# A four-layer graph network on one core: attention weights of layers 1 and 2 as the larger of a row factor and a node factor

## The chip, the cores and the metric

The kernel runs on one core of a Trainium2 chip. The metric is the device time of one execution in microseconds (us); a verdict compares medians of several executions of the kernel before and the kernel after on the same chip. The core has the engines PE (TensorE matmul, with PEld for its weight loads), DVE (VectorE), ACT (ScalarE) and POOL (GpSimd), and SP, which here only issues DMA transfers. Each engine works through its own queue in order. SBUF is the on-chip memory, PSUM the accumulators that PE writes.

## What is computed

128 graphs of 128 nodes with 128 features pass through four residual layers, each of which begins with a layer norm and a relu. `adj` holds 0 or 1, is symmetric and has a full diagonal. The change touches layers 1 and 2 alone:

```python
# layer 1, for each graph and each of 8 heads of 32 values
e   = leaky_relu(f1[:, None] + f2[None, :], 0.2)
att = softmax(where(adj > 0, e, -9e15), axis=-1)
hp  = elu(att @ h)                  # all heads side by side: xc, 256 values
h2  = xc @ W2
e2  = leaky_relu(g1[:, None] + g2[None, :], 0.2)
out = elu(softmax(where(adj > 0, e2, -9e15)) @ h2) + h_in
# layer 2
e   = leaky_relu((h @ a1) + (h @ a2).T, 0.2)
out = elu(softmax(where(adj > 0, e, -9e15)) @ h)
```

Layer 0 scores every pair of nodes, layer 3 is an attention with a bilinear score for each of 8 edge types, of which only 0 and 1 occur.

## The kernel before

The program has three stages. Stage A (profile time 0 to about 1230 us) makes layer 0's pair features. Stage B (to about 2045 us) reads them back, makes layer 0's scores and its attention, and stores `y`. Stage C, the function `layers`, finishes layer 0 and does layers 1, 2 and 3; it is the part that is changed. It exists twice, as the two arms of a run-time branch (lines 1358 to 1361): `layers(True)` where every adjacency entry is 0 or 1, `layers(False)` otherwise. The word that decides it, `types`, is made by `edge_types` in stage B from `squares`.

Stage C takes 4 graphs at a time (a group, `GC = 4`), so 32 groups, and a tile of one group has 128 partitions (nodes) by 4 x 128 values. `group(g)` is a generator that yields, step by step, the engine, an assumed cost in us, and the buffers taken and freed. `in_order` (line 54) plays all groups against these costs, with up to `UNDER_WAY = 6` of them open, and thereby fixes the order of the instructions of PE, ACT, DVE and POOL (`ORDERED`). The order is written out once; at run time each queue follows it and waits by semaphores. SP's order is not fixed by hand.

For one group before the change:

- `edges` turns the adjacency into a bf16 mask of 0 and -1 (POOL cast L1046, PE transpose L1050, DVE L1058). `with_bias` and `with_bias3` are additions on POOL (L1063, L1067). `normal_relu` is the layer norm: DVE statistics, a power on POOL (L948), DVE L951, ACT L955.
- Layer 1's heads, for each of the 4 graphs (`head_attention`): PE adds row and node terms in PSUM as an outer product of bf16 triples (L1081) and a mask term of 2^53 (L971); ACT takes the exponential twice, of the sum (L1090) and of 0.2 times it (L1091); DVE takes the larger of the two (L975 in `bounded`); PE multiplies the weights of each head with that head's values and a column of ones (L1104); DVE divides by the sum that the ones give (L1110, L1111). The bf16 triples come from DVE (L1196 to L1199, L1207).
- Layer 1's second attention and layer 2's (`single_head`) do the same with one head over the whole group: a score in PSUM (L1255, or L1281 and L1283, and L971), two exponentials (L986 or L983), the larger (L975), PE (L1019), DVE (L1026, L1028), and the elu (`positive` L1009, L998, L1002).
- The sum of the normed and the raw layer input, `x1h`, is a DVE addition (L1213).
- Layer 3 picks the score by edge type with `copy_predicated` (L1330), then two exponentials, DVE (L1336), PE (L1019), DVE (L1348), and SP stores the result (L1349). SP also loads four inputs for every group (L1039).

The tiles of the attention weights are `w` (128 x 1024, 11 buffers) for the heads and `t` (128 x 512, 28 buffers) for nearly everything else.

Of the kernel before, what the change touches and what calls it, by code (L numbers as in the profile page):

```python
# [9 lines left out]
F32 = mybir.dt.float32  # L10
# [8 lines left out]
P = 128  # L19
# [12 lines left out]
UNDER_WAY = 6  # L32
C_T, C_W, C_V, C_O, C_M = 28, 11, 3, 6, 7
C_KEPT = {"ps": 1, "t": 6, "w": 3, "v": 1}
# [6 lines left out]
SLOPE = 0.2  # L41
FAR = 2.0**53
# [120 lines left out]
def kernel(ctx: ExitStack, tc: tile.TileContext, x, adj, w, out):  # L163
# [57 lines left out]
    w2g = cst("w2g", [P, 2, P + 2])  # L221
# [18 lines left out]
    with tc.tile_pool(name="wload", bufs=2) as wl, tc.tile_pool(  # L240
# [21 lines left out]
        nc.vector.memset(fw, 0.0)  # L262
        nc.scalar.dma_start(w1c, w["L1_gnn_W1"].rearrange("h f d -> f h d"))
        a1b = wl.tile([P, NH, 2 * DH], F32, tag="a1b", name="a1b")
        nc.scalar.dma_start(a1b, bcast(w["L1_gnn_a1"], 0, P))
        for m in range(2):
# [7 lines left out]
            )  # L274

# [24 lines left out]
        for s in range(2):  # L300
# [4 lines left out]
            nc.vector.tensor_copy(w2g[:, :, P + s], gw)  # L305
# [4 lines left out]
        nc.gpsimd.dma_start(a2c, w["L2_gnn_a2"])  # L310

# [56 lines left out]
    h_d = [dram.tile([P, GB, P], F32, tag=f"h{g}", name=f"h{g}") for g in range(NB // GB)]  # L368

# [63 lines left out]
    with tc.tile_pool(name="h_pool", bufs=1) as h_pool, tc.tile_pool(name="pairs", bufs=B_V) as b_v:  # L433
# [198 lines left out]
        with tc.tile_pool(name="b2", bufs=2) as b2p, tc.tile_pool(name="b_s", bufs=2, space=PSUM) as b_s, tc.tile_pool(  # L632
# [6 lines left out]
            squares = b2p.tile([P, n_parts], F32, tag="squares", name="squares", bufs=1)  # L639

# [145 lines left out]
            def attention(k, g, u):  # L786
# [19 lines left out]
                mx = b2p.tile([P, GB], F32, tag="mx", name="mx")  # L806
                nc.vector.tensor_reduce(mx, pl, AX.X, ALU.max)
                e = b2p.tile([P, GB, P], F32, tag="e", name="e")
                nc.vector.tensor_tensor(e, pl, bcast(mx, 2, P), ALU.subtract)
                yield ACT, 0.65, "", ""  # L810
# [41 lines left out]
            def edge_types():  # L852
# [5 lines left out]
                nc.vector.tensor_scalar(odd_p, odd_p, GB * P / 4.0, None, ALU.is_gt)  # L858
                yield PE, 0.3, "pb", ""
# [16 lines left out]
            to_see, to_norm = set(range(n_parts)), set(range(n_parts))  # L876
# [25 lines left out]
    def layers(simple):  # L902

        with tc.tile_pool(name="c_in", bufs=3) as c_in, tc.tile_pool(
            name="c_t", bufs=C_T
        ) as c_t, tc.tile_pool(name="c_w", bufs=C_W) as c_w, tc.tile_pool(name="c_v", bufs=C_V) as c_v, tc.tile_pool(
            name="c_s", bufs=6
        ) as c_s, tc.tile_pool(name="c_ps", bufs=4, space=PSUM) as c_ps, tc.tile_pool(
            name="c_pz", bufs=2, space=PSUM
# [19 lines left out]
            def tile_v(name):  # L929
                return c_v.tile([P, GC, P + 3], F32, tag="v", name=name, bufs=C_O)  # L930
# [46 lines left out]
            def single_head(z, own, bias, values, ones_at, after, out):  # L977
# [13 lines left out]
                yield PE, 0.9, "pz", "t v"  # L991
                po = weighted(p, values, ones_at + 1)
                yield DVE, 0.8, "t", "pz"
# [10 lines left out]
                )  # L1004

# [25 lines left out]
            loaded = {0: early}  # L1031
# [10 lines left out]
            def edges(ad, res):  # L1042
# [8 lines left out]
                if not simple:  # L1051
# [84 lines left out]
            def group(g):  # L1136
# [80 lines left out]
                for i in range(GC):  # L1217
                    yield "fork", head_attention(i, f1d, fl, mask, vals, xh)
# [182 lines left out]
```

The softmax here doesn't subtract the row's maximum and nothing guards it: scores larger than these inputs give would overflow.

## Time and profile before

| What | Value |
|---|---|
| Runs of the kernel before | 3104.69, 3115.43, 3116.11 us; median 3115.43 |
| Span of the profiled execution | 3120.3 us |
| Mean granted TensorE clock | 0.969 |
| Stage C, first yl (L1148) to the end | 2044.5 to 3120.3 us |
| DMA in stage C, 2100 to 2900 us | 13% of the engines' time, 39 GB/s |
| DMA in stage B, slices 17 to 25 of 40 | 382 to 406 GB/s |
| SP's issues in stage C | 0.32 to 0.46 us each in the steady part |
| A 256 KB load or store in stage C, issue to landing | 2.4 to 3.1 us (medians by tensor) |

How to read it: the busy time of an engine counts the time in which at least one of its instructions is under way. A group of instructions is named by its line, engine, operation and tiles, "x" is how many there are, and a shape such as 128x512 is partitions by elements. A line that is a helper's (L948, L955, L971, L975, L1019, L1028) stands for several places in the program. An engine's instructions overlap a little, so the length of a run of equal instructions is read from the time line and not from the mean times the count.

### The profile page before, as it was taken

Reading aid. Unit: us, or ns where it says so; the run is one execution under the profiler, and the core shown is the slowest. Engines: PE = TensorE matmul, PEld = TensorE weight load, DVE = VectorE, ACT = ScalarE, POOL = GpSimd, SP = SyncE. Lnnn points to the kernel's source line nnn. Section 1 sums busy time; section 2 is a strip of 40 time slices with the busy share of each in tenths; the row PEclk is TensorE's granted clock in tenths of the full one; section 3 lists DMA queues with packets and bytes.
Section 4 is the critical chain, followed back from the end, with each engine's and each line's share of the span. In section 5 each row is a group of like instructions: output and inputs, shape, how many; then the busy total and the mean of one; then the engine's idle time right before and its main releaser. Section 6 shows DMA issues by size and latency. Waiting matters only on the chain.

```text
span 3120.3 us, 47393 instructions
## 1 busy us (share of the span) xinstructions
PE 2854.7 (91%) x17526; PEld 1595.5 (51%) x17577; DVE 2655.0 (85%) x4722; ACT 2624.7 (84%) x3050; POOL 1504.5 (48%) x972
## 2 busy tenths in 40 slices
PE   7999999999999998888888878879999999999997
PEld 3344433444334343233333333367777777787786
DVE  7999999999999998777776868768787787887886
ACT  5999999999999998887877878657877777887786
POOL 7999999999999996011111111221222222222202
PEclk9999999999999999999998989989999999999999
DMA  3655556655555550999999999630111111111000
GB/s 127 254 232 244 238 228 251 248 231 228 244 241 228 234 241 18 385 381 395 383 406 400 384 382 393 248 97 11 45 48 35 48 38 45 42 42 38 18 1 22
DMA packets 149247, 606.52 MB, mean 194 GB/s; under 512 B 14272, under 2 KB 97536, under 8 KB 118288
## 3 DMA queue, kind: packets, MB, share of 16 engines
q1 hardware_dynamic: 136128, 568.48, 46.1%
q0 software_dynamic: 10848, 33.60, 3.0%
q8 instruction: 143, 2.34, 0.3%
q10 hardware_dynamic: 2032, 1.31, 0.2%
q14 instruction: 96, 0.79, 0.1%
HBM read 322.74 MB, written 280.61 MB: 193 GB/s over the span
## 4 chain that ended last, share of the span: by engine, by line
PE 40%; DVE 32%; issue 10%; ACT 8%; POOL 6%; DMA 2%; POOLq 0%; SPq 0%; DVEq 0%; another core or an unknown queue 0%; ACTq 0%
PE ph L573 10%; DVE six L588 9%; DVE d L553 8%; PE pa L1104 6%; PE sc L707 5%; POOL d L556 4%; PE po L1019 2%; DVE p L975 2%; DMA s<-us 2%; PE ps L1123 1%; PE pl L799 1%; PE pp L1116 1%; PE pl L801 1%; PE z L971 1%; DVE v L428 1%
## 5 line engine op out<-in xcount | busy, mean ns | idle before, releaser
L556 POOL TENSOR_TENSOR d<-he 128x2016 f32<-128x2016 f32 (+1 forms) x288 | 1021.4, 3571 | 67.2 <-PE ph L573 60.2
L573 PE MATMUL ph<-d,w1T 128*64 128x512 f32 (+1 forms) x4096 | 929.0, 595 | 36.3 <-DVE us L515 13.8
L559 ACT ACTIVATE d<-d 128x2016 f32<-128x2016 f32 (+1 forms) x352 | 675.6, 1923 | 16.8 <-POOL d L556 16.7
L588 DVE BATCH_NORM_STATS2 six<-v 128x6 f32<-128x512 f32 (+1 forms) x1024 | 624.4, 669 | 6.5 <-ACT v L583 6.2
L573 PEld LDWEIGHTS ph<-d,w1T 128*64 128x64 f32 x4096 | 312.1, 136 | 539.7 <-issue 393.4
L583 ACT COPY v<-ph 128x1024 f32<-128x1024 f32 (+1 forms) x512 | 509.7, 1029 | 28.2 <-PE ph L573 26.9
L553 DVE TENSOR_TENSOR d<-he,pt 128x2048 f32<-128x2048 f32 (+1 forms) x224 | 505.4, 2257 | 2.4 <-PE ph L573 2.4
L948 POOL TENSOR_TENSOR rs<-ve,nhalf 128x4 f32<-128x4 f32 x96 | 119.2, 1241 | 737.8 <-DVE ve L945 479.5
L428 DVE SCALAR_TENSOR_TENSOR v<-v 128x1528 f32<-128x1528 f32 x256 | 433.9, 1741 | 34.2 <-ACT v L662 33.6
L662 ACT ACTIVATE v<-v,h_bi,h_sc 128x1528 f32<-128x1528 f32 x256 | 413.3, 1664 | 6.9 <-DVE h_bi L420 6.9
L707 PE MATMUL sc<-v,w_slide 128*32 128x512 f32 (+1 forms) x1536 | 324.9, 600 | 19.1 <-DVE v L428 18.7
L1104 PE MATMUL pa<-vals,p 128*128 128x99 f32 (+2 forms) x2048 | 251.7, 278 | 11.4 <-DVE p L975 7.8
L1104 PEld LDWEIGHTS pa<-vals,p 128*128 128x128 f32 x2048 | 246.9, 196 | 29.1 <-DVE p L975 11.7
L707 PE MATMUL sc<-v,w_line 128*32 128x504 f32 x512 | 260.7, 591 | 0.0
L707 PE MATMUL sc<-r,w_relu 128*32 128x504 f32 x512 | 258.2, 586 | 0.0
L975 DVE SCALAR_TENSOR_TENSOR p<-p,q 128x1024 f32<-128x1024 f32 (+1 forms) x192 | 206.9, 1084 | 50.1 <-ACT q L1091 24.4
L573 PE MATMUL ph<-both,us 128*64 128x512 bf16 x1920 | 237.7, 380 | 0.0
L573 PEld LDWEIGHTS <-us 128*64 128x64 bf16 x1920 | 125.9, 110 | 146.9 <-issue 92.2
L1090 ACT ACTIVATE p<-z 128x1024 f32<-128x1024 f32 x128 | 133.1, 1040 | 34.4 <-PE z L971 34.0
L669 ACT ACTIVATE r<-v,h_bi,h_sc 128x1008 f32<-128x1008 f32 x128 | 157.6, 1231 | 0.0
L707 PEld LDWEIGHTS sc<-v,w_slide 128*32 128x32 f32 x1536 | 65.6, 109 | 162.7 <-DVE v L428 87.0
L799 PE MATMUL pl<-u,ident 128*128 128x512 f32 x64 | 49.2, 860 | 96.6 <-POOL u L792 96.6
(275 smaller groups left out, 4490.4 us busy)
## 6 DMA issues: line engine op xcount, KB each, us to landing
v<-v SPq DMA_DIRECT2D x240, 2032.0 KB, 8.6
xg<-in_x SPq DMA_DIRECT2D x64, 256.0 KB, 3.1
ht<-h SPq DMA_DIRECT2D x64, 256.0 KB, 5.7
u<-s POOLq DMA_DIRECT2D x16, 768.0 KB, 11.8
h<-he SPq DMA_DIRECT2D x32, 256.0 KB, 2.7
adj<-in_adj SPq DMA_DIRECT2D x32, 256.0 KB, 2.9
adj<-in_adj POOLq DMA_DIRECT2D x32, 256.0 KB, 8.2
y<-yt POOLq DMA_DIRECT2D x32, 256.0 KB, 6.2
```

What stands on the lines that cost most here:

```text
L428: engine.scalar_tensor_tensor(out, v, slope, v, ALU.mult, ALU.max)
L553: nc.vector.tensor_tensor(dv, later, own, ALU.max if larger else ALU.subtract)
L556: nc.gpsimd.tensor_tensor(dv, later, own, ALU.subtract)
L559: nc.scalar.activation(d[:, 0 : 4 * n], d[:, 0 : 4 * n], AF.Abs)
L573: nc.tensor.matmul(ph[64 * a : 64 * a + 64, t, 0:n], wt, x_, start=part == 0, stop=not larger or part == 3,)
L583: nc.scalar.copy(v.rearrange("p (t e) -> p t e", t=2), ph[:, :, 0:n])
L588: nc.vector.bn_stats(made["six"][:, 2 * q + t, :], v[:, t * n : t * n + n])
L662: nc.scalar.activation(part, part, AF.Identity, bias=h_bi, scale=h_sc)
L669: nc.scalar.activation(made["r"][:, 0:n], part, AF.Relu, bias=h_bi, scale=h_sc)
L707: nc.tensor.matmul(sc[rows, 0:n], wz[:, 31 - k : 63 - k], z, start=begins and q < NQ, stop=ends and q != NQ - 1, tile_position=(0, rows.st ...
L975: nc.vector.scalar_tensor_tensor(p, p, FLOOR, q, ALU.max, ALU.max)
L1104: nc.tensor.matmul(pa_all[:, h * (DH + 1) : h * (DH + 1) + n], p[:, h, :], vals_all[:, e : e + n], start=True, stop=True,)
```

## The change

In the general arm nothing of substance changes. In the arm for adjacencies of 0 and 1:

The weight exp(leaky_relu(f1 + f2)) is the larger of exp(f1) exp(f2) and exp(0.2 f1) exp(0.2 f2). Divided by what depends on the row alone, exp(0.2 f1), and by exp(f2), which is instead multiplied into the values, it is max(exp(0.8 f1), exp(-0.8 f2)): the larger of a factor of the row and a factor of the node. The row sum divides by the same thing, so the softmax is unchanged. The kernel after computes it so:

- `exp_rows`: one small product gives the row terms and the node terms of a group (PE), ACT takes one exponential of it, SP stores the 128 x 128 result `x` to DRAM (`rows_d`), and `exp_cols` transposes it (PE) and copies the node factors out (ACT).
- The row factors are needed along the free axis on all partitions. SP reads them back from DRAM with a partition step of 0: for the heads a 128 x 1024 tile for each graph (`one_graph`, tag `R`, 9 buffers), for the other two attentions a 128 x 512 tile for each group (`one_head`).
- DVE takes the larger of that tile and the node factors, broadcast along the row. POOL multiplies by the mask, now 0 and 1 in f32. PE multiplies with the values, which POOL (`scaled_values`, `scaled_nodes`) or ACT (`second`) has multiplied by exp(f2).
- For layer 1's second attention ACT takes the exponential of 3 columns, and SP stores the row factor from SBUF as single elements into `rows_d[1]`, in place of `exp_rows`.
- `x1h` is added on POOL (`added`). `copy_predicated` uses the f32 mask.
- An empty row would now have a sum of 0. Stage B therefore keeps every row's largest score (`tops`), and `edge_types` sends the program into the general arm where one of them is below NEG/2; `types` is thus made after the last of these maxima.
- `UNDER_WAY` is 7, and the simple arm has its own numbers of buffers and its own assumed costs.

```diff
-UNDER_WAY = 6
-C_T, C_W, C_V, C_O, C_M = 28, 11, 3, 6, 7
-C_KEPT = {"ps": 1, "t": 6, "w": 3, "v": 1}
+UNDER_WAY = 7
+GENERAL_ROOM = {
+    "ps": 4, "pz": 2, "t": 28, "w": 11, "vals": 3, "f": 3, "v": 6, "mask": 7,
+}
+GENERAL_KEPT = {"ps": 1, "t": 6, "w": 3, "v": 1}
+SIMPLE_ROOM = {
+    "ps": 4, "pz": 2, "t": 26, "w": 6, "vals": 3, "v": 6, "mask": 7, "R": 9, "x": 4,
+}
+SIMPLE_KEPT = {"ps": 1, "t": 6, "w": 2, "v": 1}
...
+                mx = tops[:, g * GB : g * GB + GB]
...
+                to_top.remove(g)
+                if not to_top:
+                    yield "done", "tops"
...
+                yield "after", "tops"
+                yield DVE, 0.5, "", ""
+                low = b2p.tile([P, 1], F32, tag="low", name="low", bufs=1)
+                nc.vector.tensor_reduce(low, tops, AX.X, ALU.min)
+                nc.vector.scalar_tensor_tensor(odd_p, low, NEG / 2.0, odd_p, ALU.is_lt, ALU.max)
...
+            def attended(p, values, ones_at, after, out):
+                yield PE, 0.95, "pz", "t v"
                 po = weighted(p, values, ones_at + 1)
-                yield DVE, 0.8, "t", "pz"
+                yield DVE, 0.9, "t", "pz"
...
+            def one_head(g, k, rows, values, after, out):
+                yield DMA, 0.7, "t", ""
+                p = tile_t("p")
+                nc.sync.dma_start(p, rows)
+                yield "after", ("cols", g, k)
+                yield DVE, 0.7, "", ""
+                nc.vector.tensor_tensor(p, p, bcast(values[:, :, P + 1], 2, P), ALU.max)
+                yield "after", ("mask", g)
+                yield POOL, 0.95, "", ""
+                nc.gpsimd.tensor_tensor(p, p, masks[g], ALU.mult)
+                yield "after", ("values", g, k)
+                yield from attended(p, values, P, after, out)
+            def exp_rows(g, k, hT, weights, cols_of, scale, frees):
+                yield PE, 0.45, "ps", frees
+                pf = c_ps.tile([P, P], F32, tag="ps", name="pf")
+                for i in range(GC):
+                    nc.tensor.matmul(
+                        pf[32 * i : 32 * i + 32, :], weights, hT[:, i, :],
+                        start=True, stop=True, tile_position=(0, 32 * i),
+                    )
+                yield ACT, 0.35, "x", "ps"
+                x = c_v.tile([P, P], F32, tag="x", name="x", bufs=room["x"])
+                nc.scalar.activation(x, pf, AF.Exp)
+                yield DMA, 0.1, "", ""
+                nc.sync.dma_start(rows_d[k][g], x)
+                yield "fork", exp_cols(g, k, x, cols_of, scale)
+            def exp_cols(g, k, x, cols_of, scale):
+                yield PE, 0.2, "ps", "x"
+                px = c_ps.tile([P, P], F32, tag="ps", name="px")
+                nc.tensor.transpose(px, x, ident)
+                yield ACT, 0.3, "", "ps"
+                dst, src = cols_of(px.rearrange("p (g r) -> p g r", g=GC))
+                nc.scalar.copy(dst, src)
+                yield "done", ("cols", g, k)
+                yield from scale(g)
+            def rows_of(g, k):
+                rd = rows_d[k][g]
+                return bass.AP(tensor=rd.tensor, offset=rd.offset, ap=[[0, P], [32 * P, GC], [1, P]])
...
+                if simple:
+                    yield ACT, 0.6, "mask", "ps"
+                    mask = c_in.tile([P, GC, P], F32, tag="mask", name="mask", bufs=room["mask"])
+                    nc.scalar.copy(mask, pad)
+                    masks[g] = mask
+                    yield "done", ("mask", g)
...
+            def one_graph(i, g, cols, vals, xh):
+                yield DMA, 1.3, "R", ""
+                p = c_r.tile([P, NH, P], F32, tag="R", name="R")
+                rd = rows_d[0][g]
+                nc.sync.dma_start(
+                    p, bass.AP(tensor=rd.tensor, offset=rd.offset + 32 * P * i, ap=[[0, P], [1, NH * P]])
+                )
+                yield "after", ("cols", g, 0)
+                yield DVE, 1.25, "", ""
+                nc.vector.tensor_tensor(p, p, bcast(cols[:, 0, i, :], 2, P), ALU.max)
+                yield "after", ("mask", g)
+                yield POOL, 1.95, "", ""
+                nc.gpsimd.tensor_tensor(p, p, bcast(masks[g][:, i, :], 1, NH), ALU.mult)
+                yield "after", ("values", g, 0)
+                yield PE, 1.9, "ps", "R"
+                yield from normal_heads(i, p, vals, xh)
+            def scaled_values(g, cols, vals):
+                yield "after", ("vals", g)
+                yield POOL, 1.95, "", ""
+                by_head = vals.rearrange("p g h d -> p (g h) d")
+                nc.gpsimd.tensor_tensor(
+                    by_head, by_head,
+                    bcast(cols[:, 1].rearrange("p g h -> p (g h)"), 2, DH + 1), ALU.mult,
+                )
+                yield "done", ("values", g, 0)
+            def added(got, h1, x1):
+                yield POOL, 0.95, "t", "t t"
+                got["x1h"] = tile_t("x1h")
+                nc.gpsimd.tensor_tensor(got["x1h"], h1, x1, ALU.add)
+            def scaled_nodes(g, hv):
+                yield POOL, 0.95, "", ""
+                nc.gpsimd.tensor_tensor(
+                    hv[:, :, 0:P], hv[:, :, 0:P], bcast(hv[:, :, P], 2, P), ALU.mult
+                )
+                yield "done", ("values", g, 2)
...
+            def many_heads(g, h1, x1, h1T, vals):
+                got = {}
+                yield "fork", added(got, h1, x1)
+                cols = c_v.tile([P, 2, GC, NH], F32, tag="cols", name="cols")
+                yield from exp_rows(
+                    g, 0, h1T, fe, lambda px: (
+                        cols,
+                        px[:, :, NH : 3 * NH].rearrange("p g (k h) -> p k g h", h=NH),
+                    ), lambda _: scaled_values(g, cols, vals), "t",
+                )
+                xh = tile_w("xh").rearrange("p (g a) (b d) -> p g (a b) d", g=GC, d=DH)
+                for i in range(GC):
+                    yield "fork", one_graph(i, g, cols, vals, xh)
+                yield "join",
+                return got["x1h"], xh
...
+            def second(g, xcT, x1h, x2):
+                yield PE, 1.9, "pz v", "w"
+                h2 = tile_v("h2")
+                ph2 = by_graph(psum2("ph2"))
+                for i in range(GC):
+                    for s in range(2):
+                        nc.tensor.matmul(
+                            ph2[:, i, 0 : P + 3], xcT[:, GC * s + i, :], w2g[:, s, 0 : P + 3],
+                            start=s == 0, stop=s == 1,
+                        )
+                yield ACT, 0.3, "", ""
+                nc.scalar.activation(h2[:, :, P : P + 3], ph2[:, :, P : P + 3], AF.Exp)
+                yield "fork", one_head_rows(g, h2, x1h, x2)
+                yield ACT, 1.5, "", "pz"
+                for i in range(GC):
+                    nc.scalar.activation(
+                        h2[:, i, 0:P], ph2[:, i, 0:P], AF.Identity, scale=h2[:, i, P : P + 1]
+                    )
+                yield "done", ("values", g, 1)
+                yield "join",
+            def one_head_rows(g, h2, x1h, x2):
+                yield DMA, 0.3, "", ""
+                rd = rows_d[1][g]
+                nc.sync.dma_start(
+                    bass.AP(tensor=rd.tensor, offset=rd.offset, ap=[[1, P], [32 * P, GC]]),
+                    h2[:, :, P + 2],
+                )
+                yield "done", ("cols", g, 1)
+                yield from one_head(g, 1, rows_of(g, 1), h2, x1h, x2)
...
+                if simple:
+                    yield from exp_rows(
+                        g, 2, h2T, ae, lambda px: (hv[:, :, P : P + 2], px[:, :, 1:3]),
+                        lambda _: scaled_nodes(g, hv), "t",
                     )
-                masked(z, lambda: mask)
-                x3 = []
-                yield from single_head(z, None, shift2, hv, P, x2, x3)
+                    yield from one_head(g, 2, rows_of(g, 2), hv, x2, x3)
+                    yield "join",
...
-                    sel = by_type.pop(1)
-                    nc.vector.copy_predicated(sel, mask.bitcast(I16), by_type.pop(0))
+                    sel = by_type.pop(0)
+                    nc.vector.copy_predicated(sel, masks.pop(g).bitcast(I32), by_type.pop(1))
```

`normal_heads` is the part of `head_attention` from the product with the values on, unchanged, and `attended` that of `single_head`. The weights `fe`, `ae` and `w2g`, prepared at the start of the program, get the factors 0.8 (`RISE`) and -0.8, with some ten small DVE instructions more.

## The prediction

> **What bounds the kernel now.** I read the busy times of the stretch 2100 to 2900 us first, where stage C runs evenly, then the groups of instructions there by form, then the waits, then the time line around single POOL instructions. The stretch (us, busy time and count of PE, PEld, DVE, ACT, POOL, then granted clock, DMA share, GB/s):
>
> ```profile
> 2100.00:2900.00 800.00, 754.26 (x5646) 620.69 (x5686) 642.40 (x1735) 627.14 (x1117) 177.07 (x239) 0.98 0.13 39
> ```
>
> PE is busy for 94% of it, DVE 80%, ACT 78%, POOL 22%. The groups give the pace:
>
> ```profile
> L1104 PEld LDWEIGHTS pa<-vals,p 128*128 128x128 f32 x1568 | 190.6, 197 | 23.2 <-DVE p L975 9.9 <-issue 4.1 <-ACT val L1325 2.2
> L975 DVE SCALAR_TENSOR_TENSOR p<-p,q 128x1024 f32<-128x1024 f32 x97 | 123.1, 1272 | 19.7 <-ACT q L1091 19.1
> L1090 ACT ACTIVATE p<-z 128x1024 f32<-128x1024 f32 x98 | 101.8, 1039 | 28.1 <-PE z L971 27.7
> ```
>
> L1090 runs 4 times for a group, so 98 of them are 24.5 groups, and one takes 800 / 24.5 = 32.65 us; 32 take 1045 of stage C's 1076 us. For a group PE is busy 30.8, DVE 26.2, ACT 25.6, POOL 7.2 us. PE sets the pace. POOL has room, which its longest waits show too:
>
> ```profile
> POOL rs L948 <- DVE ve L945: 396.4, 48, 20.1
> DVE ri L1110 <- PE pa L1104: 37.2, 32, 4.1
> ```
>
> But POOL's room isn't free. Two stretches of the time line (start, length, engine):
>
> ```profile
> 2585.14 1.27 POOL L1063 TENSOR_TENSOR xg<-xg,bt_bc 128x512 f32<-128x512 f32 x1
> 2585.14 2.35 DVE L975 SCALAR_TENSOR_TENSOR p<-p,q 128x1024 f32<-128x1024 f32 x1 [2.65 <-ACT q L1091]
> ...
> 2416.90 1.21 DVE L975 SCALAR_TENSOR_TENSOR p<-p,q 128x1024 f32<-128x1024 f32 x1
> 2416.93 2.31 POOL L1063 TENSOR_TENSOR xg<-xg,bt_bc 128x512 f32<-128x512 f32 x1
> 2418.24 0.69 DVE L1028 TENSOR_TENSOR xh<-po,ri 128x512 f32<-128x512 f32 x1
> ```
>
> Where both start together, DVE's 1.22 us instruction takes 2.35: it ends 1.08 after POOL's. Where DVE is 0.03 us ahead, POOL's 1.27 takes 2.31 and ends 1.13 after DVE's. So a POOL tensor operation and a DVE operation with two SBUF inputs exclude each other, each for its length less some 0.14 us. L1028, with one input in PSUM, runs its usual 0.69 beside POOL. POOL's power L948 hardly holds anything: an L975 that began 0.41 us into one, at 2168.90, took 1.22.
>
> **The change, engine by engine, for one group.**
>
> *PE* loses L1081 and L971 (4 graphs x 4 x 0.215, the spacing in the time line, = 3.4), the score of the second attention (8 x 0.111 + 0.2 = 1.1), that of layer 2 (2 x 0.43 + 8 x 0.111 + 0.2 = 2.0) and the old row terms (0.6); it gains two row products and two transposes (2 x 0.55 = 1.1). 30.8 - 6.0 = 24.8.
>
> *ACT* loses eight exponentials of 1.04 (8.3), eight of 0.385 (3.1), two of 0.70 (1.4) and a copy (0.6); it gains the mask copy (0.6), three small exponentials and two column copies (some 0.3 each: 1.4) and four scalings of 0.39 (1.6). 25.6 - 13.4 + 3.6 = 15.8.
>
> *DVE* loses L975 (4 x 1.22 + 2 x 0.68 = 6.2), the chain L1196 to L1207 (3.1), L1213 (0.7), L1058 and L1262 (0.6); it gains the larger-of, 4 x 1.21 + 2 x 0.69 = 6.2, the same size as L975. 26.2 - 10.6 + 6.2 = 21.8.
>
> *POOL* has no row of 128x1024, nor one that multiplies two full tiles. Its rows:
>
> ```profile
> L1063 POOL TENSOR_TENSOR xg<-xg,bt_bc x32: 1262/1274/2317, 2045.2 to 2940.3; 128x512 f32<-128x512 f32 x32
> L792 POOL TENSOR_TENSOR u<-u x32: 715/717/2237, 1311.3 to 2022.8; 128x256 f32<-128x256 f32 x32
> L488 POOL TENSOR_TENSOR ln_xn<-ln_xn,ln_rs x32: 1038/1040/1042, 22.7 to 1159.9; 128x512 f32<-128x512 f32 x32
> L556 POOL TENSOR_TENSOR d<-he x288: 3547/3557/3616, 29.3 to 1225.3; 128x2016 f32<-128x2016 f32 x95, 128x2048 f32<-128x2048 f32 x49
> ```
>
> (Shortest, median, longest in ns.) L1063 and L792, both operands read in full, give (1262 - 715) / 256 = 2.13 ns an element and 0.17 us beside. L488 and L556, one operand repeated along the row, give (3557 - 1040) / 1504 = 1.67 ns and 0.18. The mask product reads both in full: 1024 x 2.13 ns + 0.17 = 2.35 us, between 1.90 (the repeated operand's rate) and 2.52 (twice L1063). So 4 x 2.35 + 2 x 1.27 (`one_head`) + 1.27 (`added`) + 1.95 (`scaled_values`, 1056 elements, repeated) + 1.04 (`scaled_nodes`) = 16.2, less two memsets of 0.1; POOL has 23.2 us in place of 7.2. The change assumes 1.95 and 0.95 for these products in its order of work.
>
> [...]
>
> *What excludes what.* DVE holds for five of 128x1024 (four larger-of, L1228) x 1.08, nine of 128x512 (two larger-of, L428, L1009 and L1002 twice, L1336, L1348) x 0.55, three small L951: 10.5 us, 17 instructions. POOL holds for 4 x 2.21 + 2 x 1.13 + 1.81 + 1.13 + 0.90, L1063 and L1067 2 x 1.13, L1046 0.47, powers 0.3: 18.0. Together 28.5 us, more than PE's 24.8. This is the new bound. At the 94% that PE reaches today it is 28.5 / 0.943 = 30.2 us. From DVE's side: an instruction finds POOL holding with a chance of 18.0 / 30.4 = 0.6 and then waits 0.84 us (half of the sum of POOL's squared holds, 30.5, over 18.0); 17 x 0.6 x 0.84 = 8.6, and 21.8 + 8.6 = 30.4. I take 30.5.
>
> *SP.* Its issues go from 5 to 14 for a group, 14 x 0.4 = 5.6 us, in one queue: behind a row load that waits for the landing of its store stand the inputs, the other groups' rows and the output. Landing: a 256 KB store 2.4 us; single elements 4.2 (256 of them, from `own_row`), so 4.2 to 8.4 for the 512 here; a row load of 512 KB between 4.6 (`a1b`, 256 KB, one source to all partitions) and 8.6 (`v`, 2032 KB). The bytes, 3.9 MB a group, are 127 GB/s against 390 in stage B. I cost all this at nothing within the stage, because 9 tiles of `R` hold two groups and 7 groups are open; without that cover it is the second rival. At the end of the program nothing covers it: the last group passes two row trips one after the other, (4.2 + 3.1 + 0.7 + 1.3) against 4.4 for L1255 to L975, and (0.8 + 2.4 + 3.1 + 0.7 + 1.3) against 4.1: 9 us.
>
> *Before the stage.* `types` is written at 2019.15 now and SP's first load follows 1.1 later. The last L807 starts at 2031.83, so `types` moves to about 2034.6 and SP to 2035.7; its 12 loads end some 8.6 later, when ACT, at 2044.5, begins the first L1148. Hidden by the norm of `y` up to there; 0 to 6 us, I take 2. The weights' ten small DVE instructions at 0.15 to 0.2: 1 us.
>
> *Sum.* 32 x (30.5 - 32.65) = -69, +9, +2, +1: 3120.3 - 57 = 3063 on the profiled execution's scale. Its span is 5 us above the runs' median, so 3058; I say **3060**. Ends: with 1.90 for the mask product the holds are 26.7, 28.3 us a group, 2988; on the other side the next paragraph.
>
> **The rivals.**
>
> *DVE and POOL in each other's way, slower.* The order fixed by hand knows nothing of the exclusion and has POOL's products too short, so POOL runs late, DVE's queue stands at a larger-of or an elu while what follows could run, and POOL in turn finds no input. DVE has 11.3 us of work that needs no exclusion. My 30.5 means that 82% of it falls in POOL's holds. With half, a group takes 21.8 + 18.0 - 5.6 = 34.2 us: 3115 + 12 + 50 = 3177. It decides against the change from 32.3 us on (32 x 0.37 = the 12 us of the other terms), that is, below 67%. For it: L951 is drawn out to 0.55 to 1.22 us already. Against: only SBUF-to-SBUF work is hit.
>
> *Row trips bind.* Six open groups at 32.65 us are 196 us for one group now. Three trips of at least 2.4 + 4.6 add 21, the longer POOL steps some 8: 225 / 7 open groups = 32.1 us, 3110, no change. Against it: much of the 196 is queueing, which shrinks.
>
> *Exclusion matters little, PE stays the bound.* 24.8 / 0.943 = 26.3 us: 3115 + 12 - 203 = 2924. It needs POOL's product at 1.4 us or below, under every row.
>
> That the program takes the general arm is excluded by the full diagonal: no row is empty, and `types` stays 0.
>
> **How the numbers follow.** Exclusion at 29 to 31.9 us a group (3010 to 3103): 0.52, time 3060. The slower rival 0.30, the trips 0.10, PE 0.08. The range leaves out PE's 0.08 and the upper third of the slower rival: 2975 to 3185; the likeliest case's own is 3010 to 3103. Half a per cent, 15 us, is about what can be told from no change: faster needs 31.8 us or less, most of the first case and PE's; slower 32.8, most of the second. That is 0.53 faster, 0.12 same, 0.35 slower.
>
> **What would show it.** POOL's 128x1024 products near 2.35 us alone and longer beside DVE; the larger-of at 1.21 alone and up to 3.4 behind one; DVE and POOL each over 90% busy in the stretch, PE near 80%. Wrong: PE still above 93%, POOL's busy time below 65%, or SP's queue behind the longest waits of DVE.

## The result, and the profile after

| | Median, us | Runs |
|---|---|---|
| before | 3112.05 | 3104.69 to 3116.11 |
| after | 3839.47 | 3822.14 to 3854.19 |

The ratio is 1.2335, 95% interval 1.2286 to 1.2384: the change makes the kernel 727 us slower. The profiled execution of after has a span of 3852.4 us. Stage C begins about where it did (first yl at 2046.15 us, before at 2044.5), so the loss lies inside it: (3852.4 - 2046) / 32 = 56.4 us a group, where the same sum gives (3120.3 - 2044.5) / 32 = 33.6 before.

The stretch of after that was shown of before, with the same columns:

```profile
2100.00:2900.00 800.00, 451.37 (x2881) 386.26 (x2880) 447.32 (x845) 243.00 (x522) 391.76 (x242) 0.75 0.31 70
```

PE falls from 94% to 56%, and no other engine takes its place: DVE 56%, ACT 30%, POOL 49%, the DMA engines 31%. Nothing is full, so something makes everything wait. The granted clock is lower too, 0.75 in place of 0.98. The page's chain of waits says who (shares of the whole span, stages A and B included):

```profile
DMA 29%; DVE 27%; PE 22%; issue 9%; POOL 7%; ACT 5%; SPq 1%; POOLq 0%; DVEq 0%; ACTq 0%
DMA e<-h 15%; DMA p<-e 9%; PE ph L600 8%; DVE six L615 7%; DVE d L580 6%; PE sc L735 4%; POOL d L583 4%; DVE R L1231 3%; DMA e<-x 2%; DMA s<-us 1%; PE pa L1208 1%; PE pl L827 1%; PE po L1113 1%; PE pl L829 1%; DVE nb L992 1%
```

`e<-h` is the store of layer 1's second attention: 512 row factors, as single elements of 4 bytes, from the column of `h2` into `rows_d[1]` (L1399). `p<-e` is the load (L1059) that reads them, or those of layer 2, back to all partitions. Together they set 24% of the whole program (some 920 us), about half of stage C. The time line of after around one such trip, all engines:

```profile
2628.53 0.36 SPq L1399 DMA_DIRECT2D e<-h  x1
...
2636.54 0.69 ACT L1523 ACTIVATE dstT<-pd,kb 128x512 f32<-128x512 f32 x1 [0.41 <-PE pt L1004]
2637.13 0.58 ACT L1007 COPY hTc<-pt 128x512 f32<-128x512 f32 x1
2649.81 0.36 SPq L1059 DMA_DIRECT2D p<-e  x1
...
2658.91 0.69 DVE L1062 TENSOR_TENSOR p<-p,h 128x512 f32<-128x512 f32 x1 [26.29 <-DMA p<-e]
2659.52 0.15 DVE L992 SCALAR_TENSOR_TENSOR nb<-mv,rs 128x4 f32<-128x4 f32 x1
2659.59 0.69 DVE L1432 TENSOR_TENSOR x<-po,xg 128x512 f32<-128x512 f32 x1
2659.68 1.27 POOL L1065 TENSOR_TENSOR p<-p,mask 128x512 f32<-128x512 f32 x1 [24.72 <-DVE nb L992]
```

SP issues the store at 2628.53, one load more, and then stands at the row load until 2649.81. The row takes another 9 us until DVE can start on it. DVE stands 26.29 us at its larger-of L1062, and behind it in DVE's queue are steps of other groups, a layer norm's (L992) and a new layer input (L1432), that ACT and POOL wait for. Between 2637.71 (the end of L1007) and 2658.91 no engine computes at all. The waits of 2300 to 3300 us add such scenes up (us in total, times, longest; SP's queue, then the engines):

```profile
SPq L1059 <- DMA e<-h: 262.3, 17, 21.8
SPq L1133 <- POOL adf L1140: 130.5, 16, 21.7
SPq L1082 <- ACT x L1080: 85.6, 14, 23.0
```

```profile
DVE p L1062 <- DMA p<-e: 377.9, 33, 26.3
POOL p L1065 <- DVE p L1062: 233.3, 25, 24.4
```

DVE stands 38% of the stretch at the larger-of of the two single-head attentions. The landings behind it, from the page's issues of DMA (KB each, median us from issue to landing, which is the last of a transfer's completion signals):

```profile
R<-e SPq DMA_DIRECT2D x128, 512.0 KB, 8.4
xg<-in_x SPq DMA_DIRECT2D x64, 256.0 KB, 3.0
...
p<-e SPq DMA_DIRECT2D x64, 256.0 KB, 8.4
...
e<-x SPq DMA_DIRECT2D x64, 64.0 KB, 5.1
...
e<-h SPq DMA_DIRECT2D x32, 2.0 KB, 18.7
```

The smallest transfer lands last: 2 KB in 18.7 us. A 256 KB row load to all partitions takes 8.4, an input of the same size 3.0. (The page can tell the landing of only a part of the transfers, of 8 of the 32 single-element stores for one.)

### The profile page after: what moved, and what is told of

Same layout as the page of the kernel before. It is cut to its first block, busy times and chain, and to the rows that moved or that the text cites. A ratio compares the mean times of both kernels' runs of the same rounds, so it can differ in the third digit from the quotient of the medians.

```text
span 3852.4 us, 45341 instructions
## 1 busy us (share of the span) xinstructions
PE 2848.7 (74%) x16489; PEld 1629.0 (42%) x16489; DVE 2793.7 (73%) x4350; ACT 2350.1 (61%) x2762; POOL 2127.8 (55%) x1196
## 4 chain that ended last, share of the span: by engine, by line
DMA 29%; DVE 27%; PE 22%; issue 9%; POOL 7%; ACT 5%; SPq 1%; POOLq 0%; DVEq 0%; ACTq 0%
DMA e<-h 15%; DMA p<-e 9%; PE ph L600 8%; DVE six L615 7%; DVE d L580 6%; PE sc L735 4%; POOL d L583 4%; DVE R L1231 3%; DMA e<-x 2%; DMA s<-us 1%; PE pa L1208 1%; PE pl L827 1%; PE po L1113 1%; PE pl L829 1%; DVE nb L992 1%
## 5 line engine op out<-in xcount | busy, mean ns | idle before, releaser
L586 ACT ACTIVATE d<-d 128x2016 f32<-128x2016 f32 (+1 forms) x352 | 675.8, 1923 | 16.5 <-POOL d L583 16.4
L1065 POOL TENSOR_TENSOR p<-p,mask 128x512 f32<-128x512 f32 x64 | 96.7, 1511 | 625.5 <-DVE p L1062 478.9
L1234 POOL TENSOR_TENSOR R<-R,mask 128x1024 f32<-128x1024 f32 x128 | 361.8, 2840 | 47.3 <-DVE R L1231 41.2
L1062 DVE TENSOR_TENSOR p<-p,h 128x512 f32<-128x512 f32 x32 | 22.6, 706 | 500.4 <-DMA p<-e 500.4
L1208 PE MATMUL pa<-vals,R 128*128 128x99 f32 (+2 forms) x2048 | 307.5, 317 | 100.4 <-DVE xh L1215 52.4
L1208 PEld LDWEIGHTS pa<-vals,R 128*128 128x128 f32 x2048 | 298.7, 232 | 118.2 <-issue 64.7
L1113 PE MATMUL po<-h,p 128*128 128x129 f32 x256 | 60.2, 409 | 318.4 <-POOL p L1065 282.2
L1231 DVE TENSOR_TENSOR R<-R,cols 128x1024 f32<-128x1024 f32 x128 | 270.1, 2133 | 14.0 <-DMA R<-e 14.0
L1113 PEld LDWEIGHTS po<-h,p 128*128 128x128 f32 x256 | 53.4, 307 | 328.4 <-POOL p L1065 289.2
```

The source lines that it names most:

```text
L586: nc.scalar.activation(d[:, 0 : 4 * n], d[:, 0 : 4 * n], AF.Abs)
L1208: nc.tensor.matmul(pa_all[:, h * (DH + 1) : h * (DH + 1) + n], p[:, h, :], vals_all[:, e : e + n], start=True, stop=True,)
L1231: nc.vector.tensor_tensor(p, p, bcast(cols[:, 0, i, :], 2, P), ALU.max)
L1234: nc.gpsimd.tensor_tensor(p, p, bcast(masks[g][:, i, :], 1, NH), ALU.mult)
```

## The experiments

"Before" beside each was 3112 to 3117 us. Each name stands for one theory in what was expected: *row trips* (the store, the row load, and SP and DVE standing at them), *exclusion* (DVE and POOL draw out each other's instructions, as in before a larger-of from 1.22 us to 2.35 and an addition on POOL from 1.27 to 2.31), and later *SP in order*, *latency* and *queue*, three ways in which a trip can cost. The runs of e5 (again), e6 and e10 are repeated; each other run is a single one, and after's own four lie 32 us apart, so a difference of that size between two single runs says little.

Where landings are counted below beyond what the page shows, they are read from the completion signals in the traces: a transfer lands with the last of its 16 signals (5 for the store of 4 rows), and transfers for which another number is on record are left out.

**e1: whole rows in place of single elements.** PE transposes the column of `h2`, ACT copies it out, and SP stores 4 rows of 512 bytes.

```diff
+                pr = c_ps.tile([GC, P], F32, tag="ps", name="pr")
+                nc.tensor.transpose(pr, h2[:, :, P + 2], ident)
...
+                nc.scalar.copy(xr[0:GC, :], pr)
...
-                    bass.AP(tensor=rd.tensor, offset=rd.offset, ap=[[1, P], [32 * P, GC]]),
-                    h2[:, :, P + 2],
+                    bass.AP(tensor=rd.tensor, offset=rd.offset, ap=[[32 * P, GC], [1, P]]),
+                    xr[0:GC, :],
```

> Layer 1's second attention stores its row factors as four whole rows of 512 bytes, after a transposition on PE and a copy on ACT, in place of 512 single elements; nothing else is changed. Theory 'row trips' (SP's queue stands behind the landing of the stores, 18.7 us for the single elements, and each group's chain passes it): the landing falls from 18.7 us to at most the 6.4 us of the 64 KB store, 12 to 16 us less for each of 32 groups, 3340 to 3460 us. Theory 'exclusion' (DVE and POOL in each other's way, the slower rival of the prediction): nothing that excludes is changed, 3800 to 3860 us.

Measured 3388.64: 451 us less than after, 14.1 us a group. The same 2 KB to the same addresses; the form of one store is the largest single cost of the change. SP's wait for it, in 2200 to 2900 us, was

```profile
SPq L1059 <- DMA e<-xr: 46.2, 12, 7.4
```

at most 7.4 us where it had been 21.8.

**e2: no trip at all for the single-head attentions.** PE spreads the row factors into PSUM, by a product with the identity, and DVE takes the larger-of from there. The heads' `R` tiles still go through DRAM.

```diff
+                    z = psum("zr")
+                    for i in range(GC):
+                        nc.tensor.matmul(z[:, i, :], *row_of(i), start=True, stop=True)
...
-                nc.vector.tensor_tensor(p, p, bcast(values[:, :, P + 1], 2, P), ALU.max)
+                nc.vector.tensor_tensor(p, z, bcast(values[:, :, P + 1], 2, P), ALU.max)
```

> The row factors of layer 1's second attention and of layer 2 are spread over the partitions by PE into PSUM (a product with a column of the unit matrix or of the factors, repeated), with no trip through DRAM; the larger-of on DVE then reads PSUM. The heads' rows still come by DMA. Row trips: the 18 us of the single-element store and the 13.8 us of the 256 KB row loads that the chain holds for a group go, and the exclusion floor of 30 to 34 us a group is left: 3080 to 3180 us. Exclusion: of 28.5 us of holds only 1.1 go, 3700 to 3860 us.

Measured 3230.13: 159 less than e1, and 50 above the window. So the two single-head trips cost 609 us together (their larger-of now reads PSUM, so that a little of the exclusion probably went with them: from 2200 to 3000 us of e2 DVE's L1168, with an input in PSUM, took 0.69 us on the mean, and L1047, which has the same shape and reads none, 1.25), and what is left is still 117 slower than before.

**e4: after without the mask products on POOL.**

```diff
-                nc.gpsimd.tensor_tensor(p, p, bcast(masks[g][:, i, :], 1, NH), ALU.mult)
...
-                nc.gpsimd.tensor_tensor(p, p, masks[g], ALU.mult)
```

> The products with the mask on POOL are left out in layers 1 and 2 (every node then counts as a neighbour); the row trips are as in the kernel after. Row trips: the chain through SP keeps its length but for POOL's 1.3 to 2.4 us steps, 3700 to 3850 us. Exclusion: 11.1 of POOL's 18 us of holds go and with them most of what was lost, 3300 us or less.

(Every node then counts as a neighbour.) Measured 3706.49, 133 less than after. Most of POOL's new work taken away, the kernel is still 593 slower than before: exclusion alone can't be the cause.

**e8: the same edit on top of e2**, with the plan, and so the order, as in e2.

> As e2_rows_by_pe with the mask's products left out on POOL (every node counts as a neighbour), the order of all else kept. Exclusion, as the second term after the row trips: POOL's holds fall from 18 to 7 us, PE's 26.6 us at 90 to 94% become the bound, 2980 to 3040 us; this is what the products on POOL cost in all, 190 to 250 us, where e4_no_masks showed 133 beside the trips. If the trips of the heads' rows are what is left: 3150 to 3230 us.

Measured 3023.74, 206 less than e2. With the single-head trips gone the products cost more than in e4; a likely reason, not tested, is that in e4 the stalls of the trips hid a part. The larger-of of 128x1024 in e2 and then in e8, 2200 to 2900 us (shortest, median, longest in ns):

```profile
L1277 DVE TENSOR_TENSOR R<-R,cols x72: 1207/2057/3386, 2242.8 to 2857.7; 128x1024 f32<-128x1024 f32 x72
```

```profile
L1275 DVE TENSOR_TENSOR R<-R,cols x99: 1209/1218/3000, 2207.3 to 2899.8; 128x1024 f32<-128x1024 f32 x99
```

The same instruction on the same data: its median goes from 2.06 to 1.22 us when POOL no longer multiplies beside it. The engines of e2 and then of e8 in that stretch:

```profile
2200.00:2900.00 700.00, 572.41 (x4095) 495.42 (x4096) 595.60 (x1133) 331.07 (x702) 505.79 (x321) 0.89 0.29 89
```

```profile
2200.00:2900.00 700.00, 637.76 (x5002) 561.12 (x5000) 583.26 (x1400) 400.22 (x856) 296.16 (x257) 0.97 0.37 115
```

e2 has no full engine (PE 82%, DVE 85%, POOL 72%); in e8 PE is the busiest again (91%). Over the whole of stage C, e2 and then e8:

```profile
2046.00:3228.00 1182.00, 951.41 (x6832) 824.53 (x6832) 994.91 (x1891) 547.10 (x1174) 862.45 (x534) 0.90 0.29 89
```

```profile
2046.00:3022.00 976.00, 880.48 (x6884) 773.09 (x6883) 794.17 (x1916) 549.10 (x1179) 388.97 (x346) 0.97 0.36 110
```

DVE has the same instructions in both, and is busy for 201 us longer beside POOL's products. It idles about as long in both (187 and 182 us). So the drawing out of DVE's instructions is nearly the whole of the 206.

**e7: e1 with the two 256 KB row loads reading `y`:** distinct addresses, and no store to wait for.

```diff
-                return bass.AP(tensor=rd.tensor, offset=rd.offset, ap=[[0, P], [32 * P, GC], [1, P]])
+                return y_d[g]
```

> As e1_whole_rows, but the two 256 KB row loads of a group take their bytes from y, the same bytes in the same pieces of 512, each address read once and not by all 128 partitions; they no longer wait for a store, and the weights of these two attentions are made of other numbers. Theory 'repeated source': a load that gives one row to all partitions is slow by itself, and the landing falls from some 8 us to the 3 us of the input loads. Theory 'queue': they are slow because they stand behind other transfers, and the landing stays above 6 us. The time, by row trips: 3200 to 3290 us, near e2_rows_by_pe, since the trips are gone; if the trips cost nothing beyond the single elements, 3340 to 3390 us.

(The weights are then made of other numbers.) Measured 3237.07, 152 less than e1, nearly e2. What is left of the trips in e1 is the row loads and the waits for their stores; the time doesn't part the two. The landings answer the other question: the 64 loads take 2.9 us at the median (shortest 2.5) in e7, against 8.7 (shortest 7.8) in e1, so a load that gives rows to all partitions is slow by itself, as the theory "repeated source" has it. In e1, 2200 to 2900 us, DVE stood for these loads:

```profile
DVE p L1062 <- DMA p<-e: 102.6, 25, 7.2
```

In the same stretch of e7 it stood once:

```profile
DVE p L1062 <- DMA p<-y: 1.0, 1, 1.0
```

**e9: after with five groups open** (`UNDER_WAY = 5`).

> The kernel after with 5 groups open in place of 7. Theory 'latency': a group's own chain with its three trips sets the pace, divided among the open groups, so stage C grows from 1807 us by 7/5 to 2530, 4500 us in all. Theory 'SP in order': the transfers of all groups pass one queue that stands still at every landing, so the pace is SP's and hardly depends on the open groups, 3800 to 4000 us.

Measured 4052.26, 213 more. A pure latency, hidden only by open groups, was to cost 660; it fits neither theory's numbers, and is nearer those of SP in order.

**e11 and e12: the same transfers, another plan.** In e11 the plan is told that 16 us pass between the store and its row load, so that other groups' transfers go between them in SP's queue; in e12 it is told of the row loads' landings too.

```diff
                 yield "done", ("cols", g, 1)
+                yield "wait", 16.0
                 yield from one_head(g, 1, rows_of(g, 1), h2, x1h, x2)
```

> The kernel after, with one number more in the plan that fixes the order: 16 us pass between the single-element store and its row load. The transfers are the same, and the store lands as late, but some ten other transfers now stand between the two in SP's queue instead of none or one. If SP's queue standing at the row load is what costs (SP in order), most of the 451 us that whole rows took off in e1 comes off here too: 3430 to 3600. If it is the group's own latency, nothing comes off: 3780 to 3900. By the exclusion alone: 3800 to 3860.

> As e11, and the plan also counts 5.5 us more for the landing of a 256 KB row load and 5 us more for a 512 KB one, so that VectorE's larger-of is put later in its queue. SP in order and VectorE behind late rows: 3300 to 3450, between e1 (3389) less the row loads' share and e2 (3230). Group latency: 3780 to 3900. Exclusion alone: 3800 to 3860.

Measured 3668.35 and 3567.18: 171 and 272 less than after, between the windows of both theories. SP standing at the load looks like a part of the cost, and not most of it (the longer plan also moves DVE's larger-of back, so the 171 aren't SP's alone). The landings of e12 show what else there is:

```profile
ht<-h SPq DMA_DIRECT2D x64, 256.0 KB, 8.2
p<-e SPq DMA_DIRECT2D x64, 256.0 KB, 14.8
...
out<-x SPq DMA_DIRECT2D x32, 256.0 KB, 7.5
e<-x SPq DMA_DIRECT2D x64, 64.0 KB, 15.4
...
e<-h SPq DMA_DIRECT2D x32, 2.0 KB, 23.9
```

Now that SP goes on issuing behind the store, other transfers land late: the 64 KB row store at 15.4 us (5.1 in after), the output at 7.5. These medians rest on 3 to 8 transfers each (18.7 and 8.4 in after on 8 and 13). Over the 59 of 64 row stores that can be told, it is 7.6 us, and over all 64 row loads 12.1 (8.8 in after): later, but not by that much.

**e15: a store that nobody waits for.** e1, with the 512 single elements stored as well, to an address that nobody reads.

```diff
+                ud = unread_d[g]
+                nc.sync.dma_start(
+                    bass.AP(tensor=ud.tensor, offset=ud.offset, ap=[[1, P], [32 * P, GC]]),
+                    h2[:, :, P + 2],
+                )
```

> e1 (whole rows are stored and read back, 3389) with the 512 single elements stored as well, from SP, to an address that nobody reads: no instruction waits for this store's data. Queue: what is issued behind it lands late all the same, so most of the 451 us comes back: 3650 to 3860. Latency of the group, or SP standing at the load that waits for this very store: nobody waits for it, so 3380 to 3460.

Measured 3704.90, 316 more than e1, 70% of the 451, though no instruction needs this store's data and the trace lists none that stood waiting for it. SP's issues in e15, and then the longest piece of the chain of waits there:

```profile
2462.36 0.46 SPq L1412 DMA_DIRECT2D n<-h  x1
2462.91 0.36 SPq L1406 DMA_DIRECT2D e<-xr  x1
2479.07 0.37 SPq L1134 DMA_DIRECT2D adj<-in_adj  x1
2484.10 0.36 SPq L1060 DMA_DIRECT2D p<-e  x1
```

```profile
2462.91 21.17 DMA e<-xr
```

The store of 4 whole rows, issued 0.55 us behind the single elements (`n<-h`), lands 21.17 us after its issue, and SP's row load waits for it. Over the 28 of 32 that can be told, this store takes 12.3 us at the median in e15, and 2.0 in e1.

**e13: e11 with the store issued by ACT**, on ACT's own DMA queue.

```diff
-                nc.sync.dma_start(
+                nc.scalar.dma_start(
```

> e11 with one edit: the single-element store is issued by ScalarE on its own DMA queue, no longer by SP. Two theories of where the 280 us went that e11 did not give back. Queue: the 512 elements stand at the head of SP's DMA queue, and what SP issues behind them (other groups' 256 KB loads, 64 KB row stores, outputs) lands after them, at 15 to 20 us in e12 in place of 2 to 3; on another queue these land early again and the time falls to 3380 to 3500. Latency or the DMA engines themselves: the store lands as late as before, the group waits as long, and the time stays at 3620 to 3720.

Measured 3703.69, 35 more than e11 and within the second theory's window: another queue doesn't help. SP's own transfers still land late (its waits, 2300 to 3300 us), while the elements' packets (queue q10; packets, MB, share of the 16 engines) take next to no DMA time:

```profile
SPq L1226 <- DMA e<-x: 102.4, 15, 21.4
```

```profile
q1 hardware_dynamic: 76230, 81.51, 38.7%
q10 hardware_dynamic: 10032, 0.04, 0.5%
```

So the delay isn't SP's queue, and by these records it isn't data time either. All packets of the store that ACT issues at 2507.20 us are on record within 2 us (2507 to 2509):

```profile
q10 hardware_dynamic: 528, 0.00, 13.1%
```

It lands 23.8 us after its issue. Each such store has 528 packets; for half of the 31 on record the last is there within 2.9 us, while the landing takes 20.5 at the median. What other transfers meet meanwhile, shown for the 64 KB row store `e<-x` (from 2100 us on; median us to landing, number of stores):

| Run | Issued while single elements are under way | Issued at other times |
|---|---|---|
| after | 16.4 (5) | 3.9 (55) |
| e12 | 17.2 (19) | 5.6 (37) |
| e13, the elements on ACT's queue | 20.0 (20) | 3.0 (31) |

A store of 64 KB on SP's queue is held up as long by elements on the other queue as by elements on its own.

By what means the elements delay it no row shows, nor does any run show why the completion of 512 elements takes so long after their packets.

**e5, e6, e10: the mask without POOL.** All are e2 with other places for the masks. e5 has one DVE instruction for the larger-of and the mask, for every 128x128 block:

```diff
-                nc.vector.tensor_tensor(p, p, bcast(cols[:, 0, i, :], 2, P), ALU.max)
...
-                nc.gpsimd.tensor_tensor(p, p, bcast(masks[g][:, i, :], 1, NH), ALU.mult)
+                for h in range(NH):
+                    nc.vector.scalar_tensor_tensor(
+                        p[:, h, :], p[:, h, :], cols[:, 0, i, h : h + 1], masks[g][:, i, :],
+                        ALU.max, ALU.mult,
+                    )
```

> As e2_rows_by_pe, and POOL no longer multiplies by the mask: DVE takes the larger-of and the mask in one instruction for each 128x128 block (32 for the heads of a group, 8 for the two others). DVE gets some 2.6 us more for a group, POOL 11.9 us less. Row trips plus exclusion as second term: DVE 24.4 us and few waits, PE 26.6 us at 94% = 28.2 us a group, 2950 to 3050 us, some 100 us below e2_rows_by_pe. If exclusion costs nothing: no gain over e2_rows_by_pe, or a loss by DVE's 2.6 us.

> The same kernel as e5_masks_on_dve, timed again beside e10: 3095 to 3115 by its first run; the question is whether it is told apart from before (3112).

e6 gives the heads' masks of three of a group's four graphs to DVE, as 128x1024 products, and those of one to POOL:

```diff
+                on_pool = i == 0
+                (nc.gpsimd if on_pool else nc.vector).tensor_tensor(
+                    p, p, bcast(masks[g][:, i, :], 1, NH), ALU.mult
+                )
```

> As e2_rows_by_pe, with the heads' masks multiplied by DVE for three of a group's four graphs (a second instruction of 1.21 us on 128x1024) and by POOL for one; the other two products stay on POOL. Exclusion with DVE as the bound of e5_masks_on_dve (93% busy there, 30.7 us a group): DVE 30.7 - 11.6 - 2.7 + 4.8 + 3.6 + 1.4 = 26.2 us, POOL 16 us, PE 26.6 us at 90%: 29.5 us a group, 2990 to 3060 us, faster than before by 2 to 4%. If DVE's instructions are held by POOL as in e2_rows_by_pe in spite of the smaller share: 3100 to 3160 us.

e10 gives all four to DVE, and keeps e5's fused form for the single heads:

> Rows spread by PE as in e2; the heads' larger-of and mask product are two VectorE instructions of 128x1024, in place of e5's eight of 128x128, the single heads keep one fused instruction for each 128x128 block, and GpSimd multiplies no mask. Two of 1.21 us in place of eight of 0.335 us save 0.26 us a graph, 1.0 us a group, 33 us in all where VectorE is the bound, as it was in e5 (93% busy): 3103 - 33, so 3040 to 3090, faster than before. If the unfused instructions pay for the exclusion with GpSimd's other tensor work (7 us a group), the saving is gone and it stays at 3100 to 3180.

| Run | Median, us | Ratio to before | 95% interval |
|---|---|---|---|
| e5 | 3103.51, again 3113.98 | 0.9997 (again) | 0.9979 to 1.0014 |
| e10 | 3128.28 | 1.0036 | 1.0023 to 1.0048 |
| e6 | 3175.17 | 1.019 | 1.0154 to 1.0226 |

All three missed the gain that was hoped for; e5 is 127 us below e2 all the same. The stretch 2200 to 2900 us of e5 (timed again), with its costliest group of instructions:

```profile
2200.00:2900.00 700.00, 610.36 (x4600) 528.85 (x4600) 634.40 (x1992) 367.78 (x786) 252.73 (x235) 0.95 0.35 108
```

```profile
L1280 DVE SCALAR_TENSOR_TENSOR R<-R,cols,mask 128x128 f32<-128x128 f32 x674 | 240.6, 430 | 3.1 <-DMA R<-e 2.5 <-ACT cols L1138 0.7
```

DVE is busy for 91% and PE for 87%. A block costs 0.43 us on the mean, so a group's 32 cost 13.8, nearly three times the heads' larger-of alone without its waits (4 x 1.21). e10's two unfused instructions, 1.21 us alone, took 1.38 and 1.43 there, on the mean, which fits a wait beside POOL's other tensor work as the larger-of had it. No version here that applies the mask beats before.

## Why the prediction was wrong

**The bound before, the work taken off, and `types`: right.** In after 1000 us (2300 to 3300) hold 1088 / 64 = 17 groups, by the weight loads of L1208. PE was busy 562.8 us there, 33.1 a group at a clock of 0.75, which is 25.3 at 0.98, an estimate that scales it by the clock (24.8 forecast). Stage C began 1.65 us later, of the 2 set down.

**The prices of single instructions: right.** POOL's mask product and DVE's larger-of in after, 2300 to 3300 us (shortest, median, longest):

```profile
L1234 POOL TENSOR_TENSOR R<-R,mask x68: 2333/2738/3421, 2312.3 to 3271.8; 128x1024 f32<-128x1024 f32 x68
```

```profile
L1231 DVE TENSOR_TENSOR R<-R,cols x68: 1209/1880/3385, 2308.9 to 3268.4; 128x1024 f32<-128x1024 f32 x68
```

2.35 us and 1.21 alone, up to 3.4 together, as worked out.

**Exclusion as the new bound: real, second in size, and under-priced.** e2 is the change with two of its three trips gone, and takes (3228.3 - 2046) / 32 = 36.9 us a group (33.6 before, by the same sum); the forecast was 30.5, the first rival's 34.2. From DVE's side the forecast had 30.4 us of work and waits for POOL; e2 shows 994.91 / 32 = 31.1, so the waits were priced about right. What failed here is that the forecast took DVE as busy all the time: it idles 16% of e2's stage, and POOL 27%. That is near the first rival's account, in which each at times stands without input because the order is fixed; and e8 gives POOL's mask products 206 us, nearly all of it as longer instructions on DVE. The 36.9 also hold the stage's beginning and end, the heads' trips and e2's own products on PE.

**The step that failed** is SP's: "I cost all this at nothing within the stage, because 9 tiles of `R` hold two groups and 7 groups are open". Three things were wrong in it. First, the price: the landing of the single elements was put at 4.2 to 8.4 us, from `own_row`, which stores 256 elements out of one partition; 512 out of 128 partitions took 18.7. The 256 KB row load was put at 3.1 in the last term of the sum, the time of an input of that size, and took 8.4 (the rival has 4.6, from `a1b`). Second, the cover: open groups hide a latency only if the queues let them pass. SP stood at the row load and DVE at L1062, each in front of other groups' work, and the core stopped (21 us in the time line above). `R`'s buffers cover the heads' loads, for which DVE waited 14.0 us in the whole of after, against 500.4 for `p`; they do nothing for `p`, which comes out of `t` and is asked for in order. Third, a landing was taken as its own affair, where one slow store delays what is issued while it is under way (e15, 316 us).

**The second rival**, "Row trips bind", named the right mechanism with a chance of 0.10 and the time 3110; its 7 us for a trip (2.4 + 4.6) compare with 27 (18.7 + 8.4) for one of the three, and it counted a trip as time in the group alone, not as time in SP's and DVE's queues. The forecast's last sentence, "SP's queue behind the longest waits of DVE", is what came, and POOL's busy time below 65% (49%) with it.

**The account**, from after's 3839, one thing removed at a time: the form of the single-element store 451 (e1), the rest of the two single-head trips 159 (e2), the mask products on POOL 206 (e8). What remains, 3024, is 88 below before: that is what the lighter work gains in a kernel that applies no mask and still has the heads' trips, and 727 = 451 + 159 + 206 - 88 (rounded). The shares depend on the order in which things are removed (the products cost 133 in e4, beside the trips). Where DVE pays for the mask (e5) the 88 are gone.

**Open:** how much of the 451 is SP's standing and how much late landings of others. e15 gives 316 for the second, with SP's standing at a row store that lands late in it; e11 gives 171 for what another order takes back; the two overlap. Also open is why the completion of the single elements comes so long after their packets. Not tried: the heads' rows spread by PE too, and the mask folded into the rows or the values.

## What to carry to other kernels

What the trips through DRAM cost here went by the shape of their packets and by what stood behind their waits, not by their bytes (2 KB in single elements landed after 18.7 us at the median of after, an input of 256 KB after 3.0): before a trip is costed at nothing, list for each queue (the issuing one, and the engine that uses the tile) which other groups' work is behind it. A store along the free axis of a few elements from each partition was better transposed on chip first here: one PE transpose and one copy were worth 451 us. And when work is moved to an engine with room, the room has to be counted together with the engine whose instructions it draws out: with POOL at 72% and DVE at 85% in e2, taking POOL's products away still saved 206 us, and DVE's larger-of fell from 2.06 us at the median to 1.22.

## What the runs showed of the hardware

- 512 single elements of 4 bytes from 128 partitions land after 18.7 us at the median and up to 30.8 (after, the 8 stores that the page can tell), although the last packet of such a store is on record within 2.9 us of its issue at the median (e13). What SP issues meanwhile lands late too, whether SP or ACT issued the elements: a 64 KB store 16.4 us in after and 20.0 in e13, against 3.9 and 3.0 at other times.
- A 256 KB load that repeats 512-byte rows to 128 partitions takes 8.7 us at the median (e1); the same load from distinct addresses, in its place, takes 2.9 (e7).
- The granted clock was lower in the stretches where PE was less busy: 0.98 at 94% busy (before), 0.97 at 91% (e8), 0.89 at 82% (e2), 0.75 at 56% (after). In the stalled kernel PE's work is slower as well: one product with the heads' values (L1104 before, L1208 in after) takes 317 ns on the mean in after and 278 before.
- Beside POOL's mask products the same work keeps DVE busy for 995 us of stage C (e2), without them for 794 (e8).
- A fused DVE instruction of 128x128 takes 0.336 us at best (e5): 2.7 us for the eight that cover 1024 elements, more than two instructions of 128x1024 (2 x 1.21).
